# The order of VectorE's work in the longer stretches of a recurrent kernel, and a bias added in four parts

## The chip, the cores and the metric

The kernel runs on one core of a Trainium2 chip. The metric is device time in microseconds. Before the change the runs gave a median of 3009.11 us, over 3 runs from 3008.05 to 3010.66.

## What is computed

Two residual layers over `x` of 64 sequences, 256 steps and 1024 features, in float32:

```python
def _L0_cond_ref(x, h0, Wx, Wh, b):
    xW = jnp.einsum('ntd,dh->nth', x, Wx) + b
    xW_t = jnp.swapaxes(xW, 0, 1)
    def step(prev_h, xw):
        next_h = jnp.tanh(prev_h @ Wh + xw)
        return (next_h, next_h)
    _, h_t = jax.lax.scan(step, h0, xW_t)
    return jnp.swapaxes(h_t, 0, 1)

# layer 0
x = x + _L0_cond_ref(x, cond_1024, L0_cond_Wx, L0_cond_Wh, L0_cond_b)
# layer 1
x = x + _L1_cond_ref(x, cond_1024, ...)
```

Layer 1 splits `v` into levels of sums and differences, multiplies all of them by one gate per sequence, `sigmoid(silu(q_pool @ W1.T + b1) @ W2.T + b2)`, and puts them together again. As every level has the same gate, that is `v * gate`, so with the layer's own `v + a` and the residual around it, `x` is multiplied by `2 + gate`. The kernel computes the gate once and then multiplies by a `factor`.

## The kernel before

The recurrence `h @ Wh` has to run step by step, 256 times. The input products `x @ Wx` do not depend on it and are made for two steps (a pair) at a time, 128 pairs in all. Between every two steps of h stands a stretch of input products for a later pair. TensorE runs one after the other: two steps, a stretch, two steps, a stretch.

A step of h (lines 1067 to 1166) is made of seven Strassen products of 32 matmuls each (`strassen_product`, L217) into the PSUM banks `m16`, `acc` and its two sisters, `main0` and `main1`. ACT copies the pre-added input `xw` into the accumulator (`put_part`, L644); VectorE adds what belongs together, ACT applies tanh, VectorE transposes. VectorE's first add of a step is L1106. `strassen_product` into `m16` comes first in a step; in the profile it is `m_h`.

The input products have float32 accuracy from products of reduced width. Each x is cut into three parts: the mask (`XWork`, L309, shown in the profile as `x_high` at L143) keeps the high bits; the difference (L325) is the piece `x2`; the low part (L320) is the piece `x1`; a cast on ACT (L331) gives `x0`. Mask, difference and low part are VectorE's, each over 128 x 1024 elements in SBUF. They are made for the next pair's x while the current pair's products run.

From pair 14 on, two pairs share part of their products by Strassen's scheme, so stretches alternate between two kinds, 57 of each. `"one"` is the longer one: 42 products of 128 x 512 into `mixed` and `main` and four chains of three products each, into the banks `chain_mixed` (tag `m57`) and `chain_main` (tag `m16`, the bank that the next step's first product uses). A chain (L954) issues its three products on TensorE, then two evictions: ACT copies `chain_mixed` negated into the sum (L820), VectorE adds `chain_main` (L823). The next chain's products overwrite or add to these banks, so they wait for the evictions of the chain before. `"two"` is the shorter one, of 39 products and no chains.

What happens when is written out by hand, in the table `at` (L1002): at product number 7 chain 5, at 14 the mask, at 16 chain 1 with what follows it (`first_two`: ACT's copy at L974, VectorE's `less_mixed` at L826, the difference), at 25 chain 6, at 28 the low part, at 34 chain 7, at 35 the first half's last eviction (`finish(0)`, L823 on `main`), `fourth_sum` (L982, VectorE) and `third_sum` (L988, GpSimd). After the products come `less_mixed` for the second half and `finish(1)`. Each engine runs its instructions in this order.

Beside this, in every stretch, GpSimd multiplies finished steps by the factor (L884) and adds the bias to the two `xw` of the next two steps when they have come back from DRAM (L790, 128 x 512 each). The sums of x go to DRAM by `store_sum` (L798) and come back by `reload_two` (L785), to change their layout; SyncE issues these transfers, the load of the next x (L888) and the stores of y (L725) in one queue. Only for the last pair the way back is in `loads_of` (L806): at step T - 4 each of the two sums is stored, loaded into `last_sums` and given its bias by one GpSimd addition over 128 x 512 (L815). The four parts of 128 x 128 of an `xw` are read one by one: ACT copies parts 0, 2 and 1 into accumulators at separate points of the step, VectorE reads part 3 at L1108.

Of the kernel before, what the change touches and what calls it, by code (L numbers as in the profile page):

```python
# [61 lines left out]
P = 128  # L62
# [3 lines left out]
G = N // R  # L66
F = D // Q
# [5 lines left out]
NP = T // S  # L73
# [19 lines left out]
def tile_cond_resid(  # L93
# [16 lines left out]
    nc = tc.nc  # L110
# [428 lines left out]
    for t in range(ALONE):  # L539
        i, s = divmod(t, S)  # L540
# [95 lines left out]
    xws = {ALONE // S: xw_next}  # L636

    def quad(v, j: int):
        return v[:, j * E : (j + 1) * E]
# [78 lines left out]
    new, slots, totals, making = {}, [], {}, ExitStack()  # L718
    forms_d = {p: [dram.tile([P, HALF], F32, tag=f"form{p}_{j}", bufs=1, name=f"form{p}_{j}") for j in range(3)] for p in range(1, 5)}

    def cols(h: int):
        return slice(h * HALF, (h + 1) * HALF)
# [4 lines left out]
    def load_step(t: int):  # L727
        steps[t] = new["pool"].tile([P, W], F32, tag="r", bufs=3, name=f"r{t}")
        return nc.sync.dma_start(out=steps[t], in_=xS[t - SWITCH])
# [42 lines left out]
    def weight(p: int, j: int):  # L772
        top, low = wx_s[FULL][j], wx_s[FULL + 1][j]
        if p in (2, 3):
            return ready[p][j][:]
        return {11: top[:, cols(0)], 1: top[:, cols(1)], 4: top[:, cols(1)], 21: low[:, cols(0)], 22: low[:, cols(1)]}[p]
# [15 lines left out]
    def store_sum(i: int, mark, steps=range(S)) -> None:  # L792
        if steps[0] == 0:
            totals["d", i] = dram.tile([S * P, W], F32, tag="sum_r", name=f"sum_r{i}")
        d, v = totals["d", i], totals[i]
        for k in range(steps[0] * G, (steps[-1] + 1) * G):
            s, g = divmod(k, G)
            dma = nc.sync.dma_start(  # L798
                out=d[s * P : (s + 1) * P, g * F : (g + 1) * F].rearrange("(q m) f -> m q f", q=Q),
                in_=v[k * R : (k + 1) * R].rearrange("m (q f) -> m q f", q=Q),  # L800
            )
            not_ahead_of(dma, mark) if k == 0 else None
        if steps[-1] == S - 1:
            del totals[i]

    def loads_of(t: int, mark) -> None:  # L806
        if t == T - 4:
            xws[NP - 1] = []
            last = split.tile([P, D], F32, tag="sum", name="last_sums")
            for s in range(S):  # L810
                store_sum(NP - 1, mark, range(s, s + 1))
                v = last[:, cols(s)]
                nc.sync.dma_start(out=v, in_=totals["d", NP - 1][s * P : (s + 1) * P])
                v = v.rearrange("p (g f) -> p g f", g=G)
                nc.gpsimd.tensor_add(v, v, new["b"][:].unsqueeze(1).broadcast_to((P, G, F)))  # L815
                xws[NP - 1].append(last[:, cols(s)].rearrange("p (i e) -> p i e", i=4))
            load_step(T - 2)

    def minus(out, mixed):
        nc.scalar.activation(out, mixed, AF.Copy, scale=-1.0)  # L820

    def plus_main(v, main) -> None:
        nc.vector.scalar_tensor_tensor(out=v, in0=main, scalar=1.0 + DOWN, in1=v, op0=ALU.mult, op1=ALU.add)  # L823

    def less_mixed(v, mixed) -> None:
        nc.vector.scalar_tensor_tensor(out=v, in0=mixed, scalar=-1.0, in1=v, op0=ALU.mult, op1=ALU.add)  # L826
# [31 lines left out]
    def beside_two(t: int, now, mark):  # L858
# [3 lines left out]
        i = (t + 1) // S  # L862
# [40 lines left out]
        def product(out, lhs, rhs, start: bool, stop: bool = False) -> None:  # L903
            nc.tensor.matmul(out=out, lhsT=lhs, rhs=rhs, start=start, stop=stop, skip_group_check=True)  # L904

        def block(j: int, k: int):
            return x[j][:, k * P : (k + 1) * P]

        def side(j: int, k: int):
            return new["s"][j][:, k * P : (k + 1) * P]  # L910
# [3 lines left out]
        def mask() -> None:  # L914
            if n + 1 < NP:
                nxt[0] = XWork(n + 1)

        def difference() -> None:
            nxt[0].difference() if nxt[0] else None
# [34 lines left out]
        def chain(p: int) -> None:  # L954
            for j in (2, 1, 0):
                if p == 5:
                    lhs, w = side(j, 0), weight(1, j)
                elif p == 1:
                    lhs, w = block(j, FULL), weight(11, j)
                elif p == 6:  # L960
                    lhs, w = side(j, 1), weight(2, j)
                else:
                    lhs, w = side(j, 2), weight(3, j)
                product(chain_mixed if j == 2 else chain_main, lhs, w, p in (5, 1) and j > 0, j != 1)
            v = {5: left[:, cols(1)], 1: left[:, cols(0)], 6: left[:, cols(1)], 7: pair_two[:, cols(0)]}[p]
            minus(v, chain_mixed)
            plus_main(v, chain_main)
# [4 lines left out]
        def first_two() -> None:  # L972
            chain(1)
            nc.scalar.copy(pair_two[:, cols(1)], left[:, cols(1)])  # L974
            less_mixed(left[:, cols(0)], mixed[0])
            difference()

        def sixth() -> None:
            chain(6)

        def fourth_sum() -> None:
            nc.vector.tensor_add(left[:, cols(1)], left[:, cols(1)], pair_two[:, cols(1)])  # L982
# [14 lines left out]
        def finish(h: int) -> None:  # L997
            plus_main(left[:, cols(h)], main[h])

        at = {}  # L1000
        if kind == "one":
            at = {  # L1002
                7: [fifth],
                14: [mask],
                16: [first_two],
                25: [sixth],
                28: [low],
                34: [seventh],
                35: [lambda: finish(0), fourth_sum, third_sum],
            }  # L1010
        elif start_of:
            at = {2 * per: [both_mixed], 5 * per: [lambda: finish(0)]}
        else:
            at = {
                lead + 2 * per: [both_mixed, mask, difference],
                lead + 4 * per: [low],
                lead + 5 * per: [lambda: finish(0)],
            }
# [48 lines left out]
    for t in range(ALONE, T):  # L1067
        i, s = divmod(t, S)
# [44 lines left out]
        elif t > T - 4:  # L1113

            v = steps[t - 1]
# [8 lines left out]
        if t >= SWITCH:  # L1124
            loads_of(t, mark)
# [24 lines left out]
        if t == T - 2:  # L1150
            residual(t, hT)
            nc.vector.tensor_mul(steps[t], steps[t], factor)
            store_step(t)
        elif last_of_group:
            group = range(first, t + 1)
            first = t + 1
            del groups[0]
            if t + 1 < SWITCH:
                later, coming = beside_x(t, later, coming, list(group), mark)
            else:  # L1160
                coming = beside_two(t, coming, mark)
        else:
            residual(t, hT)
            while behind_residual:
                behind_residual.pop(0)()
# [38 lines left out]
```

## Time and profile before

| | |
|---|---|
| median of the runs | 3009.11 us |
| profiled execution's own time | 3013.05 us |
| its span, first to last instruction | 3010.9 us |
| granted TensorE clock | 1.0 |
| mask, L143, 128 x 1024 | x127, 693 ns mean |
| difference, L325, 128 x 1024 | x127, 1542 ns mean |
| low part, L320, 128 x 1024 | x127, 1951 ns mean |
| chain evictions, L823 from chain_main | x228, 684 ns mean |
| bias adds on GpSimd, L790, 128 x 512 | x238, 1963 ns mean |
| last pair's bias adds, L815 | x2, 1285 and 1789 ns |

The busy times of a page are shares of the whole span; what a piece of work costs is seen only in the stretch where it stands, and there by who waits for it. In rows of the timeline the first number is the start in microseconds, the second the duration, then the engine (PEld is TensorE's weight load), the line, the operation, what it writes and reads, its shape, and how often it is merged in the row. Brackets show the idle time of the engine in front of it and what ended that. In rows of the waits: who waited, for whom, microseconds in total, how often, and the longest.

### The profile page before, as it was taken

What the parts mean: (1) busy time and instruction counts of PE and PEld (TensorE: products, weight loads), DVE (VectorE), ACT (ScalarE), POOL (GpSimd) and SP (SyncE); (2) the same over time, 40 slices, a digit from 0 to 9 for tenths busy, and PEclk for the clock granted to TensorE, in tenths of its full rate; (3) what the DMA queues carried; (4) which work ended last, traced back from release to release, by engine and by line L of the source; (5) the groups of instructions that cost most, each with busy time, mean ns of one, the idle gap of its engine ahead of it and who ended that gap; (6) DMA issues with size and microseconds to landing.
All of it is one profiled execution on the core that took longest, in us unless ns stands there. A gap on an engine that the chain in (4) does not pass through costs nothing.

```text
span 3010.9 us, 147296 instructions
## 1 busy us (share of the span) xinstructions
PE 2999.8 (100%) x63691; PEld 2674.2 (89%) x63691; DVE 2271.1 (75%) x5654; ACT 918.0 (30%) x2777; POOL 1034.1 (34%) x806
## 2 busy tenths in 40 slices
PE   9999999999999999999999999999999999999999
PEld 6888889988898899889988998899889988898888
DVE  7557677777777777777777777777777777777776
ACT  3223233322322333323333232232323322333222
POOL 2223333333333333333333333333343333433332
PEclk9999999999999999999999999999999999999999
DMA  7335554454445544544445445444454444444543
GB/s 266 129 123 174 167 162 141 145 169 157 142 147 160 164 141 143 167 156 148 142 154 172 143 142 158 160 153 141 153 173 145 143 153 159 159 141 146 172 153 111
DMA packets 266891, 464.87 MB, mean 154 GB/s; under 512 B 30224, under 2 KB 103952, under 8 KB 266256
## 3 DMA queue, kind: packets, MB, share of 16 engines
q1 hardware_dynamic: 266112, 454.94, 46.9%
q8 instruction: 513, 8.40, 1.2%
q14 instruction: 122, 1.00, 0.1%
q10 hardware_dynamic: 144, 0.52, 0.1%
HBM read 316.93 MB, written 138.41 MB: 151 GB/s over the span
## 4 chain that ended last, share of the span: by engine, by line
PE 97%; DMA 2%; DVE 0%; POOL 0%; SPq 0%; issue 0%; ACT 0%; DVEq 0%; POOLq 0%
PE main L904 24%; PE acc L217 22%; PE m_h L217 15%; PE main_h L217 14%; PE mixed L904 13%; PE chain_main L904 3%; PE chain_mixed L904 2%; PE main L296 1%; PE mixed L296 1%; DMA x<-xT 1%; PE m L217 1%; DMA wh<-wh 0%; DMA h0T<-condT 0%; DMA w<-w1T 0%; POOL sum L342 0%
## 5 line engine op out<-in xcount | busy, mean ns | idle before, releaser
L884 POOL TENSOR_TENSOR r<-r,factor 128x512 f32<-128x512 f32 x238 | 329.9, 1386 | 1324.8 <-DVE r L651 1029.1
L904 PE MATMUL main<-wx,x 128*128 128x512 f32 x3156 | 772.1, 389 | 0.0
L904 PEld LDWEIGHTS main<-wx,x 128*128 128x128 f32 x3156 | 592.5, 188 | 123.4
L790 POOL TENSOR_TENSOR xw<-xw,b_h 128x512 f32<-128x512 f32 x238 | 465.3, 1963 | 305.1 <-DMA xw<-sum_r 290.3
L1080 ACT ACTIVATE h<-h 128x128 f32<-128x128 f32 x992 | 280.0, 306 | 531.9 <-DVE h L1106 318.4
L904 PE MATMUL mixed<-wx,x 128*128 128x512 f32 x1578 | 402.5, 399 | 0.0
L904 PEld LDWEIGHTS mixed<-wx,x 128*128 128x128 f32 x1578 | 286.9, 188 | 79.4 <-issue 23.8
L644 ACT COPY acc<-xw 128x128 f32<-128x128 f32 x738 | 188.2, 267 | 537.4 <-POOL xw L790 445.4
L1084 DVE STREAM_TRANSPOSE hT<-h 128x128 f32<-128x128 f32 x988 | 302.7, 306 | 41.8 <-ACT h L1080 40.0
L217 PE MATMUL acc<-t,hT 128*32 128x128 f32 x8160 | 270.6, 273 | 1.8 <-issue 1.2
L217 PE MATMUL acc<-wh,s 128*32 128x128 f32 x8160 | 271.8, 273 | 0.0
L217 PE MATMUL acc<-wh,hT 128*32 128x128 f32 x8160 | 269.7, 273 | 0.0
L217 PE MATMUL main_h<-t,s 128*32 128x128 f32 x7936 | 266.1, 273 | 0.0
L217 PE MATMUL m_h<-wh,hT 128*32 128x128 f32 x7936 | 265.2, 274 | 0.5 <-ACT u L1123 0.2
L217 PE MATMUL main_h<-wh,s 128*32 128x128 f32 x7936 | 264.3, 273 | 0.3 <-issue 0.3
L217 PE MATMUL m_h<-t,s 128*32 128x128 f32 x7936 | 264.0, 273 | 0.0
L820 ACT ACTIVATE sum<-chain_mixed 128x512 f32<-128x512 f32 x228 | 136.5, 599 | 414.5 <-PE chain_mixed L904 351.8
L320 DVE TENSOR_TENSOR x<-x,x_high 128x1024 fp32r<-128x1024 f32 x127 | 247.7, 1951 | 5.3 <-PE main L296 5.2
L217 PEld LDWEIGHTS m_h<-wh,hT 128*32 128x32 f32 x7936 | 211.8, 110 | 44.2 <-DVE sum L823 16.5
L217 PEld LDWEIGHTS acc<-t,hT 128*32 128x32 f32 x8160 | 227.9, 110 | 3.6 <-issue 1.8
L217 PEld LDWEIGHTS acc<-wh,s 128*32 128x32 f32 x8160 | 230.3, 110 | 0.0
L217 PEld LDWEIGHTS acc<-wh,hT 128*32 128x32 f32 x8160 | 227.7, 110 | 0.3
(135 smaller groups left out, 3989.2 us busy)
## 6 DMA issues: line engine op xcount, KB each, us to landing
wx<-form SPq DMA_DIRECT2D x342, 256.0 KB, 6.0
x<-xT SPq DMA_DIRECT2D x127, 512.0 KB, 4.3
sum_r<-sum SPq DMA_DIRECT2D x484, 128.0 KB, 2.2
r<-xS SPq DMA_DIRECT2D x241, 256.0 KB, 5.7
yS<-r SPq DMA_DIRECT2D x241, 256.0 KB, 5.4
xw<-sum_r SPq DMA_DIRECT2D x240, 256.0 KB, 4.9
ahead<-xT SPq DMA_DIRECT2D x57, 128.0 KB, 4.5
wh<-wh SPq DMA_DIRECT2D x8, 512.0 KB, 10.7
```

Of the source, the lines that this page charges most:

```text
L217: nc.tensor.matmul(out=out[q * R : (q + 1) * R], lhsT=a[:, k * R : (k + 1) * R], rhs=wh_s.sides[i][k][:, q], start=first and k == 0, stop= ...
L296: nc.tensor.matmul(out=acc[h], lhsT=v[:, k * P : (k + 1) * P], rhs=wx_s[k][which][:, h * HALF : (h + 1) * HALF], start=start and k == 0, s ...
L320: nc.vector.tensor_sub(self.x1, x, self.high)
L644: nc.scalar.copy(part, xws[t // S][t % S][:, j])
L790: nc.gpsimd.tensor_add(v, v, new["b"][:].unsqueeze(1).broadcast_to((P, G, F)))
L820: nc.scalar.activation(out, mixed, AF.Copy, scale=-1.0)
L884: nc.gpsimd.tensor_mul(steps[r], steps[r], factor)
L904: nc.tensor.matmul(out=out, lhsT=lhs, rhs=rhs, start=start, stop=stop, skip_group_check=True)
L1080: nc.scalar.activation(quad(h, j), quad(h, j), AF.Tanh)
L1084: nc.vector.transpose(quad(hT, j), quad(h, j))
```

## The change

In stretches of kind `"one"`, the mask of the next x moves from product 14, where it stood ahead of chain 1, to the end of `first_two`, behind chain 1's eviction and `less_mixed`. The difference moves from there to the end of `sixth`, behind chain 6's eviction. VectorE's order was: chain 5's eviction, mask, chain 1's eviction, `less_mixed`, difference, chain 6's eviction, low part, chain 7's eviction. It becomes: chain 5's eviction, chain 1's eviction, `less_mixed`, mask, chain 6's eviction, difference, low part, chain 7's eviction. TensorE's, ACT's, GpSimd's and SyncE's instructions in these stretches keep their order.

For the last pair, each of the two bias additions over 128 x 512 becomes four over 128 x 128, in the order of parts 0, 2, 1, 3.

```diff
@@ loads_of
                 nc.sync.dma_start(out=v, in_=totals["d", NP - 1][s * P : (s + 1) * P])
-                v = v.rearrange("p (g f) -> p g f", g=G)
-                nc.gpsimd.tensor_add(v, v, new["b"][:].unsqueeze(1).broadcast_to((P, G, F)))
-                xws[NP - 1].append(last[:, cols(s)].rearrange("p (i e) -> p i e", i=4))
+                v = v.rearrange("p (i e) -> p i e", i=4)
+                for j in (0, 2, 1, 3):
+                    nc.gpsimd.tensor_add(v[:, j], v[:, j], quad(new["b"], j % 2))
+                xws[NP - 1].append(v)
             load_step(T - 2)
@@ beside_two
             chain(1)
             nc.scalar.copy(pair_two[:, cols(1)], left[:, cols(1)])
             less_mixed(left[:, cols(0)], mixed[0])
-            difference()
+            mask()
 
         def sixth() -> None:
             chain(6)
+            difference()
@@
         if kind == "one":
             at = {
                 7: [fifth],
-                14: [mask],
                 16: [first_two],
                 25: [sixth],
                 28: [low],
```

## The prediction

> **What bounds the kernel now.** I read the page's busy times first.
>
> ```profile
> PE 2999.8 (100%) x63691; PEld 2674.2 (89%) x63691; DVE 2271.1 (75%) x5654; ACT 918.0 (30%) x2777; POOL 1034.1 (34%) x806
> ```
>
> TensorE is busy for the whole span and the chain of waits lies 97% on it. VectorE's work is free until TensorE waits for it. So next come the waits, cut to the rows that name the evictions and the mask:
>
> ```profile
> DVE x_high L143 <- DMA x<-xT: 140.3, 112, 4.1
> ...
> PEld m_h L217 <- DVE sum L823: 16.5, 46, 0.6
> ...
> PEld chain_main L904 <- DVE sum L823: 4.8, 12, 0.9
> ```
>
> The 140.3 us in front of the mask is idle VectorE time; the 16.5 us at m_h looks like a loss and mostly is none. I took the 57 longer stretches one by one from the timeline, each from the first product of L904 to the first m_h product behind it. The shortest lasts 12.463 us, 38 of 57 are within 0.01 of it, and the same 0.35 us of idle weight loading stands before m_h there as in the others. 54 products at a pitch of 0.227 us are 12.24, so 12.463 hides no large wait. All 57 sum to 714.4 us, 57 x 12.463 is 710.4: TensorE loses **4.0 us** there in all. That is the whole prize for the VectorE edit.
>
> **How VectorE and GpSimd share.** A stretch as it is now (starting at 437.94; all times from here on are counted from a stretch's start):
>
> ```profile
> 443.03 0.69 DVE L143 TENSOR_SCALAR x_high<-x 128x1024 int32<-128x1024 int32 x1 [1.58 <-DMA x<-xT]
> 443.64 0.68 DVE L823 SCALAR_TENSOR_TENSOR sum<-chain_main,sum 128x512 f32<-128x512 f32 x1
> 444.36 0.69 DVE L826 SCALAR_TENSOR_TENSOR sum<-mixed,sum 128x512 f32<-128x512 f32 x1
> 444.58 1.29 POOL L790 TENSOR_TENSOR xw<-xw,b_h 128x512 f32<-128x512 f32 x1 [2.64 <-DMA xw<-sum_r]
> ...
> 444.97 1.99 DVE L325 SCALAR_TENSOR_TENSOR x<-x_high,x 128x1024 fp32r<-128x1024 f32 x1
> ...
> 446.38 1.73 POOL L790 TENSOR_TENSOR xw<-xw,b_h 128x512 f32<-128x512 f32 x1 [0.50 <-DMA wx<-form]
> 446.88 0.68 DVE L823 SCALAR_TENSOR_TENSOR sum<-chain_main,sum 128x512 f32<-128x512 f32 x1
> 447.48 1.71 DVE L320 TENSOR_TENSOR x<-x,x_high 128x1024 fp32r<-128x1024 f32 x1
> 449.11 0.68 DVE L823 SCALAR_TENSOR_TENSOR sum<-chain_main,sum 128x512 f32<-128x512 f32 x1
> ```
>
> See the difference (L325): alone it takes 1.22 us elsewhere, here 1.99. It ends 1.08 after the bias add's end (445.87). Then the second add takes 1.73 and not 1.29: it ends 1.15 after the difference's end (446.96). Then the low part (L320) ends 1.08 after that add. So operations whose operands are all in SBUF take turns with GpSimd, whole instructions at a time; evictions (L823, L826), which read PSUM, stay at 0.68 beside the same adds. The mask belongs to the first kind:
>
> ```profile
> 159.08 0.69 DVE L143 TENSOR_SCALAR x_high<-x 128x1024 int32<-128x1024 int32 x1
> 159.25 1.68 POOL L524 TENSOR_TENSOR x<-x,factor 128x512 f32<-128x512 f32 x1 [4.83 <-DVE x L654]
> ```
>
> The GpSimd operation ends 1.15 after the mask. With these two figures (a VectorE turn ends 1.08 after GpSimd's, GpSimd's 1.15 after VectorE's; the next VectorE instruction starts 0.08 before an end), with the adds' starts as seen, I get 1.71 for L320 and nearly every chain 7 eviction of now within 0.02 us.
>
> **When a late eviction costs.** Stretch 1598 shows it:
>
> ```profile
> 1610.70 0.68 DVE L823 SCALAR_TENSOR_TENSOR sum<-chain_main,sum 128x512 f32<-128x512 f32 x1
> ...
> 1611.43 0.59 PEld L217 LDWEIGHTS m_h<-wh,hT 128*32 128x32 f32 x24 [0.64 <-DVE sum L823]
> ```
>
> m_h (the same bank as chain_main) starts 0.73 after the start of chain 7's eviction. So that eviction is free up to 12.46 - 0.73 = 11.73, and each later us costs one. Chain 6's eviction holds chain 7's products; stretches with it at 9.35, 9.40, 9.44 are 0.09, 0.18, 0.23 too long, so it is free up to about 9.24. Chain 1's holds chain 6's products, 2.72 earlier: free up to about 6.5.
>
> **The change part by part.** *Mask (one of 0.69 us per stretch), moved behind L826.* Chain 1's eviction no longer stands behind a mask that waits for x: it starts at 5.50, the earliest seen, in all stretches. The late ones (x landing at 6.5 to 6.7 in the stretches at 1272, 1319, 2480: 0.69 to 0.88 us each) and those late at chain 6 are healed: **-4.0 us**, all the stalls of now. The mask can start at 6.83. There lies the first bias add: it starts at 5.93 to 7.80, median 6.75. Until now the mask had ended before every one of these adds; its old cover, VectorE's idle time, is gone.
>
> *Difference (one per stretch), moved behind chain 6's eviction (8.27 at the earliest).* It then stands directly ahead of the low part, and the second add (median start 8.20) lies in the way of one or the other. Chain 7's eviction, finish(0), L982, L826, finish(1) and the next step's first add (L1106) queue behind. Three cases, over the 57 stretches:
> - First add before 6.83: 33 stretches. At 437.94: first add 6.64 to 7.93, mask ends 8.48 (+0.55, its 0.69 less the 0.14 that precedes a turn), second add to 9.72, eviction of chain 6 at 8.40, difference ends 9.72 + 1.08 = 10.80, low 11.94, chain 7's eviction 11.86 instead of 11.17: 0.13 lost. Over the 33: 3.1 us, mean 0.09.
> - Mask first, then both adds: 13. At 1691.73: mask 6.83 to 7.52, adds end 8.67 and 9.99, difference 11.07, low 12.21, eviction 12.13: 0.40 lost. Over the 13: 5.2 us.
> - Mask first, second add after 8.88: 11. At 2758.95: difference 8.88 to 10.10, second add to 11.25, low 12.33, eviction 12.25: 0.52 lost. Over the 11: 5.7 us.
>
> Together **+14.0 us** where 4.0 were lost. The unknown is whether a mask waits for an add that has begun: no row shows it. If not (row: 0.69 always), the same sum gives 7.9. I take that it waits, since it is seen to hold GpSimd off and the difference, its nearest row, shows both directions. 0.1 us on chain 7's eviction, either way, makes 14.0 into 10.0 or 18.5.
>
> The Trainium skill, "SBUF — State Buffer", section "Who interferes with whom", has it that `tensor_scalar` in its 2-port mode and VectorE instructions with two SBUF inputs contend with GpSimd, and that whoever issues first keeps the shared pair for the whole instruction. That speaks against the change: it puts all three such operations among GpSimd's two adds, where one had passed them by. By the page the mask waits (14.0); by the row of a mask alone it doesn't (7.9).
>
> *Costed at nothing.* x0's cast (L331) runs at about 14 and the mask ends by 8.7. The low part frees x's buffer about a us later, and its next load is issued some 13 us on. ACT reads the first add's result from about 10.8, and that add ends by 9.1; the second's is read a step later. No DMA is moved on any queue, no product either, and GpSimd's order stays. Behind a late m_h, finish(1) ends 2.66 after m_h's start, L1106 needs it at 2.97: 0.3 to spare.
>
> *Bias by quadrants*, at the end of the program only:
>
> ```profile
> 2988.82 1.79 POOL L815 TENSOR_TENSOR last_sums<-last_sums,b_h 128x512 f32<-128x512 f32 x1 [11.83 <-DMA last_sums<-sum_r]
> ...
> 2990.64 0.27 ACT L644 COPY acc<-last_sums 128x128 f32<-128x128 f32 x1 [2.65 <-POOL last_sums L815]
> ...
> 2990.85 0.26 ACT L1123 COPY u<-m_h 128x128 f32<-128x128 f32 x1
> ...
> 2991.16 1.08 PE L217 MATMUL m_h<-wh,hT 128*32 128x128 f32 x32 [0.24 <-ACT u L1123]
> ```
>
> Products of 32 matmuls follow each other at 0.87 us, so m_h would start at 2990.66 and lost 0.50, the next product at 2992.57 another 0.54: 1.04. GpSimd's 128x128 operations (L834) take 0.456 and follow at 0.41. The first quadrant is done at 2989.3, the four at 2990.5, no later than the one add now. The first copy no longer waits, and all of it can go; at worst the 1.19 us that TensorE idles at 2999.75 on "issue" grow by it. Between -1.04 and 0 I take **-1.0**, as the chain of waits runs through that add.
>
> **Sum:** 14.0 - 4.0 - 1.0 = **+9.0 us**. The profiled execution took 3013.05 (span 3010.9 and 2.2 around it), so 3022 on its own scale. The median of the runs is 3009.11, 3.9 lower; 9.0 above it is **3018**.
>
> **Rivals.**
> *The mask doesn't wait for an add.* For: every mask in the trace is 0.65 to 0.70. Against: none began more than 0.04 us behind a GpSimd operation. 7.9 - 4.0 - 1.0 = +2.9: 3012, no change. Chance 0.14.
> *The adds come early enough* (not slower): bank waits healed, nothing new. It decides where chain 7's eviction stays under 11.73. Were both adds 0.6 us earlier, 4.5 us would be lost instead of 14.0; with none lost it is -4.0 - 1.0 = 3004. For: a launch without the profiler may move data sooner. Against: 42 of 57 pass 11.73. Chance 0.12.
> *The second add falls between difference and low every time*, the dearest case: 57 x 0.52 = 29.6, so +24.6: 3034. For: a later eviction of chain 6 invites it. Against: 45 of the 57 second adds start before 8.88. Chance 0.13.
>
> **From these to the numbers.** Forecast 0.56, as above; 0.05 for something else. 3009 to 3026 holds the forecast with its errors and the first rival, and leaves the ends of the other two out. About 0.2% (6 us) can be told from no change. Slower by more: 0.52 of the forecast, 0.03, 0.13, 0.02, so 0.70. Same: 0.04, 0.11, 0.07, so 0.22. Faster: 0.05 of the second rival and 0.03, so 0.08.
>
> **What would show it.** The mask at about 6.8, 1.2 to 1.8 us long where an add has begun; chain 1's eviction at 5.50 everywhere; no chain_main row in TensorE's waits; chain 7's eviction at a median of 11.9, m_h 0.73 behind it, longer stretches summing to some 724 us; no ACT wait of 2.65 at 2990. I am wrong if the mask stays 0.69 beside an add, or if the adds themselves start elsewhere than now.

## The result, and the profile after

The changed kernel takes 3017.35 us (median of 7 runs, 3016.62 to 3022.23); before took 3009.34 us beside it (7 runs, 3008.05 to 3010.66). The ratio is 1.0029, with a 95% interval from 1.0018 to 1.0041: slower by 8 us. The profiled execution took 3016.68 us, its span is 3014.4 us.

The busy times of the page after:

```profile
PE 2999.1 (99%) x63691; PEld 2675.0 (89%) x63691; DVE 2278.8 (76%) x5654; ACT 918.7 (30%) x2777; POOL 994.4 (33%) x812
```

TensorE does the same work in a longer span. VectorE is 7.7 us busier with the same number of instructions, GpSimd 39.7 us less busy: VectorE now waits more for GpSimd, and GpSimd less for VectorE, and such a wait stands in the rows as a longer instruction. The waits after (lines of the code are one or two higher from L817 on):

```profile
DVE x_high L143 <- DMA x<-xT: 41.6, 54, 4.0
...
PEld m_h L217 <- DVE sum L824: 28.7, 57, 1.0
```

VectorE hardly waits for x any more (41.6 us instead of 140.3; what is left is in other stretches), and no row names chain_main's products as waiting. The row at m_h has grown from 16.5 to 28.7, and now all 57 longer stretches are in it. As in the profile before, 0.35 us of each is no loss: 28.7 - 57 x 0.35 = 8.7. Measured from first product to m_h, the 57 stretches add up to 719.17 us, 8.8 over 57 x 12.463. Two ways of reading give one number.

The stretch at 437.39, in which the first bias add begins ahead of the mask (timeline of the changed kernel):

```profile
444.13 2.99 POOL L790 TENSOR_TENSOR xw<-xw,b_h 128x512 f32<-128x512 f32 x2 [2.75 <-DMA xw<-sum_r]
444.22 1.75 DVE L143 TENSOR_SCALAR x_high<-x 128x1024 int32<-128x1024 int32 x1
...
445.90 0.68 DVE L824 SCALAR_TENSOR_TENSOR sum<-chain_main,sum 128x512 f32<-128x512 f32 x1
446.50 1.71 DVE L325 SCALAR_TENSOR_TENSOR x<-x_high,x 128x1024 fp32r<-128x1024 f32 x1
448.13 1.21 DVE L320 TENSOR_TENSOR x<-x,x_high 128x1024 fp32r<-128x1024 f32 x1
449.26 0.68 DVE L824 SCALAR_TENSOR_TENSOR sum<-chain_main,sum 128x512 f32<-128x512 f32 x1
...
449.99 1.08 PE L217 MATMUL m_h<-wh,hT 128*32 128x128 f32 x32
```

The mask, 0.69 us in every row of before, takes 1.75 here: it waits for an add that began 0.09 us ahead of it. The difference then waits for the second add, the low part is free, chain 7's eviction starts 11.87 us into the stretch, and m_h 0.73 behind it, at 12.60. The prediction had worked out 11.86 for the same pattern.

The stretch at 1088.66, in which the mask is first:

```profile
1095.49 0.68 DVE L143 TENSOR_SCALAR x_high<-x 128x1024 int32<-128x1024 int32 x1
1095.62 2.94 POOL L790 TENSOR_TENSOR xw<-xw,b_h 128x512 f32<-128x512 f32 x2 [2.96 <-DMA xw<-sum_r]
...
1097.55 2.10 DVE L325 SCALAR_TENSOR_TENSOR x<-x_high,x 128x1024 fp32r<-128x1024 f32 x1
1099.57 1.21 DVE L320 TENSOR_TENSOR x<-x,x_high 128x1024 fp32r<-128x1024 f32 x1
1100.70 0.68 DVE L824 SCALAR_TENSOR_TENSOR sum<-chain_main,sum 128x512 f32<-128x512 f32 x1
...
1101.44 1.08 PE L217 MATMUL m_h<-wh,hT 128*32 128x128 f32 x32 [0.24 <-DVE sum L824]
```

The mask keeps its 0.68, both adds come later, and the difference takes 2.10. The eviction is at 12.04, 0.17 later than in the first pattern, although the mask was done 1.07 us earlier.

The end of the program, with the bias in quadrants:

```profile
2994.25 1.74 POOL L816 TENSOR_TENSOR last_sums<-last_sums,b_h 128x128 f32<-128x128 f32 x4 [14.39 <-DMA last_sums<-sum_r]
2994.74 0.27 ACT L644 COPY acc<-last_sums 128x128 f32<-128x128 f32 x1 [3.71 <-POOL last_sums L816]
...
2994.94 0.26 ACT L1124 COPY u<-m_h 128x128 f32<-128x128 f32 x1
...
2995.25 1.19 PE L217 MATMUL m_h<-wh,hT 128*32 128x128 f32 x32 [1.40 <-ACT u L1124]
```

ACT's first copy follows the start of the adds by 0.49 us, where it was 1.82. Yet TensorE waits longer here than before, 1.40 us: the stored sums took 4.0 us to land in DRAM in this execution and 3.4 to come back (2.2 and 2.85 before). One execution can't tell whether the change does that; the runs below bear on it.

### The profile page after: what moved, and what is told of

Its sections match the earlier page's. It is cut to its first block, busy times and chain, and to the rows that moved or that the text cites. A ratio compares the mean times of both kernels' runs of the same rounds, so it can differ in the third digit from the quotient of the medians.

```text
span 3014.4 us, 147249 instructions
## 1 busy us (share of the span) xinstructions
PE 2999.1 (99%) x63691; PEld 2675.0 (89%) x63691; DVE 2278.8 (76%) x5654; ACT 918.7 (30%) x2777; POOL 994.4 (33%) x812
## 4 chain that ended last, share of the span: by engine, by line
PE 95%; DVE 2%; DMA 2%; POOL 0%; issue 0%; ACT 0%; SPq 0%; DVEq 0%; POOLq 0%; ACTq 0%
PE main L905 23%; PE acc L217 22%; PE m_h L217 15%; PE main_h L217 14%; PE mixed L905 13%; PE chain_main L905 3%; PE chain_mixed L905 2%; PE main L296 1%; DVE x L320 1%; PE mixed L296 1%; PE m L217 1%; DVE sum L824 1%; DMA wx<-form 0%; DMA wh<-wh 0%; DMA h0T<-condT 0%; DMA w<-w1T 0%
## 5 line engine op out<-in xcount | busy, mean ns | idle before, releaser
L790 POOL TENSOR_TENSOR xw<-xw,b_h 128x512 f32<-128x512 f32 x238 | 424.6, 1793 | 304.9 <-DMA xw<-sum_r 294.4
L824 DVE SCALAR_TENSOR_TENSOR sum<-chain_main,sum 128x512 f32<-128x512 f32 x228 | 156.5, 686 | 139.7 <-ACT sum L821 139.3
L217 PEld LDWEIGHTS m_h<-wh,hT 128*32 128x32 f32 x7936 | 211.9, 110 | 53.6 <-DVE sum L824 28.7
```

What stands on the lines that cost most here:

```text
L217: nc.tensor.matmul(out=out[q * R : (q + 1) * R], lhsT=a[:, k * R : (k + 1) * R], rhs=wh_s.sides[i][k][:, q], start=first and k == 0, stop= ...
```

## The experiments

The theory was: a mask, a difference or a low part takes turns with GpSimd's adds, instruction by instruction; in their new places VectorE's three meet both adds, chain 7's eviction is late by that, and m_h behind it. The first rival: VectorE simply has too much to do between the evictions, whoever else works. The second: the loss comes from the end of the program.

**The order alone.**

```diff
-                for j in (0, 2, 1, 3):
-                    nc.gpsimd.tensor_add(v[:, j], v[:, j], quad(new["b"], j % 2))
+                v = v.rearrange("p (g f) -> p g f", g=G)
+                nc.gpsimd.tensor_add(v, v, new["b"][:].unsqueeze(1).broadcast_to((P, G, F)))
```

> VectorE's new order alone; the last pair's bias is added in one piece as before. Theory (VectorE's moved operations take turns with GpSimd's two bias adds, so chain 7's eviction is late and m_h with it): the 57 longer stretches add up to 719 us or a little more (712 to 715 with the old order), chain 7's eviction at a median of 11.85, the time 6 to 10 us over before. Rival (the loss comes from the bias in four pieces at the program's end): as before, 3009.

3019.19 us (5 runs, 3018.54 to 3019.73), ratio to before 1.0035 [1.0023, 1.0048], 11 us over the 3008.24 of before beside it and one more than the 6 to 10 expected. The longer stretches add up to 721.86 us, chain 7's eviction has its median at 11.93. The second rival falls: all of the loss comes with the order.

**The quadrants alone**, the other half of the same diff on the kernel before.

> The bias of the last pair by quadrants alone; VectorE's old order. Theory: the first copy of ACT starts 0.5 us behind the start of the bias adds instead of 1.8, the time is 0 to 1.5 us under before. Rival (the loss lies here): 3 to 8 us over before.

3007.38 us (11 runs, 3005.72 to 3010.26), 0.9 under before; ratio 0.9996 [0.9987, 1.0005], so the gain is not told from none by the times. The trace shows what happens. First the kernel before once more (the run `before_again` below), then this one, both from the timeline:

```profile
2982.76 1.73 POOL L815 TENSOR_TENSOR last_sums<-last_sums,b_h 128x512 f32<-128x512 f32 x1 [11.44 <-DMA last_sums<-sum_r]
2984.52 0.27 ACT L644 COPY acc<-last_sums 128x128 f32<-128x128 f32 x1 [2.48 <-POOL last_sums L815]
...
2985.04 1.08 PE L217 MATMUL m_h<-wh,hT 128*32 128x128 f32 x32 [0.28 <-ACT u L1123]
```

```profile
2982.59 2.23 POOL L816 TENSOR_TENSOR last_sums<-last_sums,b_h 128x128 f32<-128x128 f32 x4 [11.08 <-DMA last_sums<-sum_r]
2983.55 0.27 ACT L644 COPY acc<-last_sums 128x128 f32<-128x128 f32 x1 [1.68 <-POOL last_sums L816]
...
2984.41 1.18 PE L217 MATMUL m_h<-wh,hT 128*32 128x128 f32 x32
```

From the start of the adds to ACT's copy it is 0.96 us instead of 1.76, and the bracket at m_h is gone. From the last stretch to the program's end the two executions take 32.27 and 31.60 us.

**No bias adds in the longer stretches.**

```diff
-            reload_two(i, places, False, lambda: store_step(t - 1))
+            reload_two(i, places, kind == "one", lambda: store_step(t - 1))
```

> The changed kernel without GpSimd's two bias adds in the longer stretches; it leaves the bias of those steps out of the sum. Theory (turns with GpSimd): mask 0.69, difference and low part 1.22 each in all 57, chain 7's eviction at 11.16, stretches at 12.463 each and 710.4 in all, the time 7 to 9 us under the changed kernel, about 3009 or a little less. Rival (too much VectorE work ahead of chain 7's eviction, whoever else works): chain 7's eviction stays over 11.7 and the time at 3017.

3004.54 us (11 runs, 3003.87 to 3006.53), ratio to before 0.999 [0.9981, 0.9999], 13 us under the changed kernel; 7 to 9 had been expected. One of the 13 is a difference between the two sets of runs: before took 3008.24 beside this run and 3009.34 beside the changed kernel. Of the 11.8 us between the two profiled spans, 8.8 lie in the longer stretches, 1.1 in the end of the program and 2.0 in the steps of h; why those 3.1 differ stays open. The stretches add up to 710.41, as expected: none is over 12.481. The stretch at 437.42:

```profile
444.25 0.68 DVE L143 TENSOR_SCALAR x_high<-x 128x1024 int32<-128x1024 int32 x1
...
446.30 1.22 DVE L325 SCALAR_TENSOR_TENSOR x<-x_high,x 128x1024 fp32r<-128x1024 f32 x1
447.43 1.22 DVE L320 TENSOR_TENSOR x<-x,x_high 128x1024 fp32r<-128x1024 f32 x1
448.57 0.68 DVE L824 SCALAR_TENSOR_TENSOR sum<-chain_main,sum 128x512 f32<-128x512 f32 x1
...
449.88 1.08 PE L217 MATMUL m_h<-wh,hT 128*32 128x128 f32 x32
```

Same order, same VectorE instructions, no bias add beside them: 0.68, 1.22 and 1.22, the eviction at 11.15, 0.58 within its free limit of 11.73. The first rival falls. In the stretches the order by itself loses nothing; it even heals what before lost.

**Before, once more, for its profile.**

> The kernel before, once more, for its profile on this chip. The profile shown of before came from an execution 4 us over its median. If its late x loads were the reason, the stretches add up to 711 to 713 us here instead of 714.4; if not, the difference lies between the stretches or at the end.

3006.58 us. The stretches add up to 712.05: 1.7 us are lost there, not 4.0. One stretch (at 1317) has x land at 6.46 and loses 0.66; the three late x loads of the first profile are mostly chance. The run of the quadrants alone, with the old order too, lost 2.0. 2.3 of the 6.3 us between the two spans lie here; of the rest, 1.95 and 1.75 lie in the steps behind the two kinds of stretches. The prediction's sum was made against an execution that lost more than is usual.

**The second bias add behind `third_sum`**, in the changed kernel:

```diff
-        for v in places if not biased else []:
-            ...
+        for v in places[:first] if not biased else []:
+            add_bias(v)
...
             nc.gpsimd.tensor_add(pair_two[:, cols(1)], pair_two[:, cols(1)], pair_two[:, cols(0)])
+            add_bias(places[1])
```

(`first` is 1 in stretches of kind `"one"`, else 2; `add_bias` holds the two lines that stood in the loop.)

> The changed kernel with the second bias add of each longer stretch moved on GpSimd behind third_sum, where VectorE is done with the x. Theory (two turns of GpSimd are needed to make chain 7's eviction late; with one, the sum of turns gives it at 11.2, under the free limit of 11.73): mask still 1.2 to 1.8 us long where the first add has begun, but difference and low part 1.22 each, chain 7's eviction at 11.2 to 11.5, stretches 710.4 to 711 us in all, time 3004 to 3007, under both kernels. Rival (one add is enough): stretches over 715 and time over 3012.

3007.06 us (11 runs, 3005.98 to 3008.21), ratio to before 0.9991 [0.9983, 1.0], 10 under the changed kernel; the expected upper end was 3007, the stretches are at 710.53. The stretch at 438.5 (lines differ by a few from the other kernels'):

```profile
445.30 1.29 POOL L783 TENSOR_TENSOR xw<-xw,b_h 128x512 f32<-128x512 f32 x1 [2.79 <-DMA xw<-sum_r]
445.35 1.78 DVE L143 TENSOR_SCALAR x_high<-x 128x1024 int32<-128x1024 int32 x1
...
447.66 1.21 DVE L325 SCALAR_TENSOR_TENSOR x<-x_high,x 128x1024 fp32r<-128x1024 f32 x1
448.79 1.21 DVE L320 TENSOR_TENSOR x<-x,x_high 128x1024 fp32r<-128x1024 f32 x1
449.93 0.68 DVE L827 SCALAR_TENSOR_TENSOR sum<-chain_main,sum 128x512 f32<-128x512 f32 x1
...
453.18 1.29 POOL L783 TENSOR_TENSOR xw<-xw,b_h 128x512 f32<-128x512 f32 x1
```

The mask still gives up 1.1 us to the first add, but with the second add 7.9 us behind the first the difference and the low part run alone. The latest eviction of chain 7 in all 57 is at 11.42. One turn of GpSimd is covered, two are not. This version is clearly faster than the changed kernel; against before its interval ends at 1.

**The same on the kernel before**, in VectorE's old order:

> The kernel before with the second bias add moved in the same way; VectorE's old order. Theory: chain 7's eviction at 10.93, but late x loads and evictions of chain 6 stay, so stretches 711 to 713 us (712.05 now), time within 2 us of before. It tells whether the gain of the run beside it belongs to the second add's place alone (then this one is as fast) or needs the new order as well.

3009.33 us (11 runs, 3007.16 to 3013.41), ratio 1.0002 [0.9993, 1.0011]; stretches 711.74. With the old order the second add's place is worth nothing that can be told. The run above, 2.3 us under this one beside the same runs of before, has both.

**The mask back at product 14**, the difference left behind chain 6's eviction:

```diff
             less_mixed(left[:, cols(0)], mixed[0])
-            mask()
...
                 7: [fifth],
+                14: [mask],
```

> The changed kernel with the mask back at product 14, ahead of chain 1; the difference stays behind chain 6's eviction. Theory: both adds are now past the mask, and the second meets the difference or the low part: chain 7's eviction at 11.5 to 11.8, 7 to 11 us lost in the stretches (717 to 721 in all), time 3013 to 3017, so the difference's move costs most of it. Rival (the mask's new place is the whole cause): stretches 712, time 3008.

A miss: 3011.87 us (10 runs, 3009.7 to 3014.01), ratio 1.0009 [1.0, 1.0018], and 715.81 in the stretches, below the 3013 to 3017 and the 717 to 721 expected, and above the rival's 3008 and 712. 5.4 us are lost; chain 7's eviction is over 11.73 in 16 stretches, where the changed kernel has 42. Put the starts of the adds as this run's own trace has them into the prediction's rule of turns, and it gives 5.2. The rule held, the starts were others. The difference alone costs some 4 us (5.4 less the 1.7 of before's second profile), mask and difference together 7 to 10.

**The difference back ahead of chain 6's eviction**, behind the mask's new place:

```diff
             mask()
+            difference()
...
             chain(6)
-            difference()
```

> The changed kernel with the difference back ahead of chain 6's eviction, right behind the mask's new place. Theory: first add, mask, second add and difference now take turns ahead of chain 6's eviction, which comes at 9.7 to 10.5 where 9.24 is free: 45 to 57 us lost in the stretches (755 to 768 in all), time 3050 to 3062. Rival (an eviction of chain 6 behind the difference is harmless, as it was before): time at 3008 to 3017.

3062.8 us (4 runs, 3060.23 to 3065.44), ratio 1.0178 [1.0164, 1.0192]; the stretches add up to 766.35. That is 53 us over before, a little past the 3062 expected at most. Chain 6's eviction has its median at 10.37, and its waits have moved to the chain that follows:

```profile
PEld chain_main L905 <- DVE sum L824: 62.8, 57, 1.8
...
PEld m_h L217 <- DVE sum L824: 20.2, 57, 0.4
```

The row at m_h is back at 57 x 0.35: chain 7's products start late as well, so its eviction is not what ends last. The changed kernel avoids this by its second move; the same turns cost it six times less, because they fall ahead of an eviction with more room.

## Why the prediction was right, point by point

**Time and direction.** 3018 was forecast, 3017.35 measured, with +9.0 forecast and +8.0 measured. The mechanism is the forecast's own, and the run without adds shows it: the same order without the adds loses nothing in the longer stretches.

**The mask waits for an add.** No row of before showed it, and the forecast took it from the nearest row. It does: 1.75 us in the stretch shown, a median of 1.54 over the 57. The rival with 3012 is out, but by these rows and not by the time: its price was too low. In the forecast's second and third case the mask comes first and waits for nothing, and these two alone are 5.2 + 5.7 = 10.9 us. The 7.9 comes out only if the mask doesn't hold the adds up either, and the row at 159.08 shows that it does. So the rival stood at 3015 or more, which the time hardly tells from 3018. The Trainium skill, "SBUF — State Buffer", section "Who interferes with whom", names `tensor_scalar` in its 2-port mode and operations with two SBUF inputs as contending with GpSimd, the first to issue keeping the pair. The rows agree: an add 0.09 us ahead of the mask costs it 1.07, and evictions, with one input in PSUM, stay at 0.68 beside both adds. That the mask runs in such a mode, no row shows. The forecast's own wording, "operations whose operands are all in SBUF", is too wide: the transposes of h (L1084) read and write SBUF, and the 67 that began during a GpSimd operation in the kernel before took 0.31 us, like the others.

**The rule of turns and the free limit.** From the starts of both adds in the changed kernel's own trace, the rule gives 8.8 us lost; 8.8 were measured. In all but one stretch the length is 12.463 or the start of chain 7's eviction plus 0.73, within 0.02 us.

**The term +14.0 was mis-sized**, at 8.8 in the profiled execution and 11.5 in the run of the order alone (721.86 - 710.39). The step that was off is the third case, "Mask first, second add after 8.88: 11". It came true in 3 stretches each (1.2 and 1.6 us, instead of 5.7). The forecast took the adds' starts as they were in the old order, and in 5 of the 11, its example at 2758.95 among them, the old order had made the start late:

```profile
2765.78 1.21 DVE L325 SCALAR_TENSOR_TENSOR x<-x_high,x 128x1024 fp32r<-128x1024 f32 x1
2765.92 4.45 POOL L790 TENSOR_TENSOR xw<-xw,b_h 128x512 f32<-128x512 f32 x2 [2.98 <-DMA xw<-sum_r]
```

The difference, at its old place from 6.83 on, holds the first add until 9.20, and the second follows from 9.16. The change takes the difference away from there. So it was in 8 of 9 such stretches of before's second profile, and in none of the 3 and 3 with the new order; what is left of the case are late loads. The first case had 39 and 29 stretches at 0.07 and 0.06 (0.09 forecast), the second 15 and 25 at 0.32 (0.40 forecast, because I let the second add start 0.03 behind the first one's end and it starts 0.04 ahead of it). How the 57 fall into the first two cases hangs on the landing of transfers to within 0.1 us (the first add's median start is 6.72 and 6.80, the mask's 6.83), and one execution does not fix that.

**The term -4.0 was mis-sized too.** The stalls of before were 1.7 in a second execution and 2.0 in the run of the quadrants alone. That they are healed is right: chain 1's eviction starts by 5.74 everywhere. Both errors together: 14.0 - 4.0 was forecast, 8.8 to 11.5 less 1.7 was found, 7.1 to 9.8. They nearly cancel, and that is part of why the time came out so near.

**The quadrants, -1.0.** ACT's copy comes 0.8 to 1.3 us sooner behind the adds' start; the time is 0.9 lower alone, and the changed kernel is 1.8 under the order alone, though not run beside it. The size fits, but the interval of the run with quadrants alone includes no change. The longer landing in the changed kernel's profile is not the quadrants' doing: the store's second half, issued 5.30 us behind the last stretch, lands at 9.29 there and at 9.00 in the run of the order alone, but at 7.49 in the run of the quadrants alone; the four other runs with quadrants don't have it either. With it, the end from the last stretch on takes 33.06 and 33.87 us, in the eight other executions 31.60 to 32.59. That is about a microsecond of the loss that the forecast did not have, and its cause stays open.

## What to carry to other kernels

An instruction moved to where its engine was free also moves to where another engine was at work. Before such a move, look at what the second engine runs at the new place, and whether the two take turns; count the turns against the room of the first instruction that someone waits for. And a gap of an engine that recurs in the shortest stretches too is no loss: measure stretches against the shortest, not by the sum of waits. Last, a start that is read from the old order may be an effect of that order: ask what it waited for before it goes into a sum for the new one.

## What the runs showed of the hardware

Recorded starts tell which of VectorE and GpSimd goes first down to some 0.05 us: in the changed kernel an add that starts at 6.79 makes a mask at 6.83 wait, one at 6.85 waits for it. Below that they don't: in the kernel before, a GpSimd operation at 136.79 waited for a mask at 136.83. Back to back, they alternate: of two VectorE instructions in a row, a waiting add gets the turn between them, and costs the second a whole turn, as in the stretch at 948.51, where the low part took 2.31 us instead of 1.21 and 0.68 us were lost.
